# A sparse graph-attention block: hub stage, second-layer step order and norms rearranged

## The chip, the cores and the metric

The kernel runs on one core of a Trainium2 chip. Its time is the device time in microseconds of one launch, taken as the median over several runs. The core has a matrix engine (TensorE, PE in the profile; PEld is its weight load), VectorE (DVE), ScalarE (ACT), GpSimd (POOL) and SyncE (SP, which only issues transfers here). Each engine works through its own instructions in program order and waits on semaphores for the others. Transfers are issued from SP's, ACT's and POOL's queues.

## The reference

x is [8, 2048, 64]: 8 graphs over the same 2048 nodes with 64 features. adj is a 2048 x 2048 0/1 matrix that is very sparse, except that the first nodes (the hubs) have many neighbours. In essence:

```python
def gat(h, mask, b):                       # h: [..., N, D]
    scores = einsum('nd,md->nm', h, h)
    scores = where(mask, scores, -1e16)
    return einsum('nm,md->nd', softmax(scores), h) + b

mask = adj + eye(N) > 0
h   = einsum('bnc,hdc->bhnd', x, Wh)       # 4 heads of 64
z   = leaky_relu(concat_heads(gat(h, mask, bh)), 0.2)
h2  = einsum('bnk,dk->bnd', z, Wo)         # back to 64
z2  = leaky_relu(gat(h2, mask, bo), 0.2)
out = layernorm(x + (layernorm(z2) * gamma + beta))   # both without further weights
```

## The kernel before, in words

The kernel never forms the dense 2048 x 2048 attention. It splits the nodes into 56 hubs (HUB) and 1992 others, the others into 166 sets of 12 (SET, NS). For each set it finds the at most 128 nodes that are a neighbour of any of the 12, gathers just their rows, and computes a 128-wide attention with a mask. Hubs are done densely, in blocks of nodes. The 8 graphs are handled as 4 pairs (Q = 4), each pair side by side on the 128 partitions or columns.

All is emitted under `tc.manual_schedule()` (L1401): every engine runs its instructions in the order in which the Python code emits them, and only the waits are worked out. So the order of the lines is the order of the work. Four stages follow one another.

**Hub stage** (loop L958, 16 blocks i of 128 nodes). Before it, ACT's queue loads the x tiles 0 to 3 (`load_x`), SP's queue loads hub rows, weights and the first adjacency pieces; `hub_mask` and `hub_mask_sets` (L539, L556) build the hub masks maskh and maskt with PE transposes, `weights` turns the weight matrices, `hub_columns` makes the hubs' score columns yh. In each block `load_x(i + 4)` loads ahead, `more` loads adjacency pieces `raw` of 480 KB on SP and converts them on POOL to `a`, `save_x` writes the x tile to table1 on SP; then for two halves t, `hub_scores` (PE sh L590, DVE subtract e L594, ACT exp L597), the next block's transposes, `hub_values` of the half before (PE oh L608). `make_keys` (PE pk L721, DVE keys L708) packs adjacency columns into sort keys at fixed blocks; `pick` makes the list of selection jobs (DVE MAX8 and match-replace L737/739, index list, masks), of which `some(3)` runs three per half. When the list is empty the first gathers from table1 (POOL indirect transfers, L792) are issued.

**First layer** (loop L1017, steps i over 83 groups of two sets). A step computes scores of group i+1, values of group i, the output projection of i-1, second-layer maps of i-2 and rows of i-3, in one software pipeline. `keep_rows` (L892) adds the bias and stores the rows to table2 with two transfers on SP. `second_maps` and `second_rows` use corners of the step's PSUM tile `cat`.

**Passage and second layer** (loop L1351, steps u over NU = 42 groups of four sets). 24 gathers from table2 go out first (L1100), and tiles bd, es2, esh, ownb, linked are made and cleared on DVE (L1103 to L1117). `hub_block` (L1262) loads 120 rows of table2 for a hub block on SP. A step u emits, in this order:

- `scores2(u+2)` (PE s L1133, ACT exp into eT L1136); `values2(u)` (PE o L1165). Two steps share one o tile, and after the odd one `spread` puts that pair's norm jobs on the steps ahead.
- for a hub block, `hub_values2` (PE oh L1299); four gathers for u+6; `work_on(u, 0)`: the norm jobs of this step's first half; `roots(u)`: ACT Ln and Exp for the variances; `hub_lift2` (DVE L1285, ACT exp L1288) for the block whose scores were made the step before; `spread_own(u+3)`: ACT copies the sets' own columns into bd (L1124).
- `turn_scores(u+1)` (PE e L1144) and `keep_scores` (DVE es L1152); `turn2(u+4)`: two PSUM tiles with 8 transposes each (PE t L512), each copied by ACT to xTg (L1320); for a hub block `hub_scores2` (PE sh L1277); `work_on(u, 1)`.

Hub blocks fall on every second step from u = 2 (`hub_at`, L1346). The tiles of `turn2` and of `hub_scores2` share the tag "T", with two buffers in PSUM:

```python
tp = bank2(f"t2_{g}", "T", 2)             # turn2, two per step
sp = held["sh", b] = bank2(f"sh2_{b}", "T", 2)   # hub_scores2, read in hub_lift2
```

A norm (L1171) is: reciprocal and product with the softmax sums (`first`), leaky (`act`), sum, centre with a square on ACT, variance; scale, times gamma, plus the residual (`again`); and a second mean, centre, variance, scale and store. The jobs lie on eight successive steps, each list as (first half, second half):

```python
return [([], [first, act, mean(0)]), ([centre(0)], []), ([var(0)], []), ([], [again, mean(1)]), ([centre(1)], []),
        ([], []), ([var(1)], []), ([end], [])]
```

**End**: the loop runs seven steps past the last values so that the norms finish; eight stores per norm go out on SP (the last norm's partly on ACT). A flag tells whether a dense fallback must run; it doesn't here.

Of the kernel before, what the change touches and what calls it, by code (L numbers as in the profile page):

```python
# [359 lines left out]
def fast_kernel(ctx: ExitStack, tc: tile.TileContext, x, adj, Wh, bh, Wo, bo, gamma, beta, out, flag):  # L360
# [54 lines left out]
    wnat = early.tile([P, H, C], F32, name="wnat")  # L415
    whT = early.tile([P, H * D], F32, name="whT")
    gram = early.tile([P, H, P], F32, name="gram")
    wos = early.tile([D, H * D], F32, name="wos")
# [30 lines left out]
    def load_x(i):  # L449
        t = xrow[i] = rows_tile(f"x{i}")  # L450
        nc.vector.memset(t[:, :, 0:PW:PW - 1], 1.0)
        for p in range(2):
            nc.scalar.dma_start(out=t[:, :, 1 + p * D:1 + (p + 1) * D],
                                in_=x[p::2, i * P:(i + 1) * P, :].rearrange("q n c -> n q c"))
# [32 lines left out]
    number = early.tile([P, 2, HALFN], U16, name="number")  # L487
    nc.gpsimd.iota(number, [[1, 2], [2, SEG // 2], [SEG, HALFN // (SEG // 2)]], base=0, channel_multiplier=0)
    load_x(2)
    load_x(3)  # L490
# [18 lines left out]
    def turn(tp, rows):  # L509

        for q in range(Q):
            nc.tensor.transpose(tp[:, q * P:(q + 1) * P], rows[:, q, 1:1 + P], ident)  # L512
# [24 lines left out]
    HV = HW // 4  # L537

    def hub_mask():  # L539
# [3 lines left out]
        pm = two("pm")  # L543
# [3 lines left out]
        for k in range(2):  # L547
            nc.vector.tensor_scalar(
                maskh[:, k * 8:(k + 1) * 8, :].rearrange("p m (n h) -> p (m n) h", h=H),
                pm[:, k, :8 * HUB].unsqueeze(2).to_broadcast([P, 8 * HUB, H]), 0.0, 255.0, OP.is_equal, OP.mult)  # L550
# [5 lines left out]
    def hub_mask_sets():  # L556
        pm = two("pms")
        cols = early.tile([HUB, NS * SET], BF16, tag="a", name="hubs", bufs=5)
        nc.scalar.copy(cols.rearrange("n (s k) -> n s k", k=SET), hubm[:, HUB:].rearrange("n (k s) -> n s k", s=NS))
# [9 lines left out]
    yh = early.tile([P, 2, 2 * HUB * H], F32, name="yh")  # L569
# [29 lines left out]
    hubo = [two(f"oh{t}", "o") for t in range(2)]  # L599
# [63 lines left out]
    keys = [early.tile([P, HALFN], F32, name=f"keys{k}") for k in range(2)]  # L663
    cand = early.tile([P, SEG * KEEP], F32, name="cand")
    best = early.tile([P, P], F32, name="best")
# [226 lines left out]
    def keep_rows(g, pr):  # L892
# [3 lines left out]
        for j in range(2):  # L896
            nc.sync.dma_start(out=dst[2 * g + j], in_=r[j * 48:(j + 1) * 48])
# [41 lines left out]
    more(2)  # L939
    hub_mask()  # L940
    hub_mask_sets()
    weights()
    turn_x(0)
    hub_columns()
    picks = []

# [7 lines left out]

    for e in es:
        nc.vector.memset(e[:, 4 * HW:], 1.0)
    pend = None
    for i in range(NB):  # L958
        if i + 4 < NB:
            load_x(i + 4)  # L960
        more(2 if i < 7 else 1)
        save_x(i)
# [12 lines left out]
        for t in range(2):  # L975
# [6 lines left out]
            if t == 1 and i in (3, 6):  # L982
                make_keys(0, (i - 3) // 3, two)
                if i == 6:
                    picks = pick(0)
            if t == 1 and i in (9, 15):
                make_keys(1, (i - 9) // 6, two)
            some(3)
    hub_values(*pend)
    while picks:  # L990
        picks.pop(0)()
    LOOK = 5
    for g in range(LOOK - 2):
        for j in range(2):
            gather(table1, 2 * g + j, 1, rows_tile)
# [16 lines left out]

    picks = pick(1)
# [3 lines left out]
    for i in range(-4, NG + 3):  # L1017
# [6 lines left out]
        cat = one(f"cat{i}", "C")  # L1024
# [15 lines left out]
        if i + 6 < NG and i % 2 == 0 and i >= -2:  # L1040
            own_rows((i + 6) // 2)
        if 0 <= (i - 30) // 2 <= NV:
# [18 lines left out]
        if 0 <= i - 2 < NG:  # L1061
            second_maps(i - 2, cat[:, 0, 384:384 + GM])
        if 0 <= i - 3 < NG:
            second_rows(i - 3, cat[:GM, 1, 384:512])
        if 0 <= i + 4 < NG + NG % 2:
            columns(i + 4, cat)
        if 0 <= i - 2 < NG:
            keep_own(i - 2, cat[:, 0, 384:384 + GM])
        if 0 <= i - 3 < NG:
            keep_rows(i - 3, cat[:GM, 1, 384:512])  # L1070
# [13 lines left out]
    assert not picks and not pieces and not todo3 and done == NS  # L1084
# [13 lines left out]
    NU = (NS + 3) // 4  # L1098
    sets = [list(range(4 * u, min(4 * u + 4, NS))) for u in range(NU)]
# [3 lines left out]
    bd = [late.tile([P, 4, Q, 32], F32, name=f"bd{k}", bufs=1) for k in range(3)]  # L1103
    es2 = [late.tile([P, 2 * Q, 4, 32], F32, name=f"es2_{k}", bufs=1) for k in range(2)]
    esh = [late.tile([P, Q * 2 * HUB + 8], F32, name=f"esh{k}", bufs=1) for k in range(2)]
# [328 lines left out]
```

## Time and profile before

| | us |
|---|---|
| median of 9 runs | 880.39 (876.9 to 882.74) |
| the profiled execution | 878.06 |
| its span | 876.2 |
| mean granted PE clock | 0.957 |

| stage of the profiled execution | from | to |
|---|---|---|
| hub stage | 0 | 144.5 |
| first layer | 144.5 | 599.0 |
| passage to the second layer | 599.0 | 609.1 |
| second layer, up to the last values o | 609.1 | 843.83 |
| end | 843.83 | 876.2 |

The profile is of one execution. Each line of a group or of the timeline names the source line, the engine, the operation and the tiles (out<-in); a bracket at its end tells how long the engine was idle before it and what released it. In a row of stages stand the length, then the busy time of PE, PEld, DVE, ACT and POOL with the number of instructions, the granted PE clock, the share of DMA engines busy and GB/s.

### The profile page before, as it was taken

The page shows a single profiled execution, that of the slowest core. Times are in us where ns is not written, and L with a number is a line of the kernel's source. Part 1 is how long each engine was busy: PE and PEld are TensorE (multiplying, and loading weights), DVE is VectorE, ACT ScalarE, POOL GpSimd, SP SyncE. Part 2 cuts the span into 40 slices and gives each one's busy share as a digit, 9 for nine tenths or more (in the row PEclk, how much of TensorE's full clock was granted, in tenths as well). Part 3 has the DMA queues.
Part 4 walks back from the last instruction along what each step waited for, and adds up shares of the span by engine and source line. Part 5 has one row for each costly group of instructions (what it writes and reads, how often), then busy time and mean ns, then how long its engine had stood idle before and what let it go on. Part 6 is the DMA issues. An engine that isn't in the chain of part 4 may idle for free.

```text
span 876.2 us, 42066 instructions
## 1 busy us (share of the span) xinstructions
PE 748.6 (85%) x18437; PEld 657.4 (75%) x18437; DVE 610.1 (70%) x1369; ACT 514.1 (59%) x961; POOL 467.9 (53%) x612
## 2 busy tenths in 40 slices
PE   2895677889999999999999999993999999998730
PEld 2663456778778999988999999971889999988720
DVE  3346983568888778877655555553258999999994
ACT  2342333546556667666666667651677788887821
POOL 6643141448344546655666665503777777777300
PEclk9999999999999999999999999995999999999975
DMA  8787441356344445665566565513888888888611
GB/s 188 222 218 209 130 145 51 83 141 173 97 108 112 114 127 156 168 168 153 157 168 172 160 167 160 132 31 117 243 259 253 271 283 269 269 241 257 173 46 36
DMA packets 81794, 145.22 MB, mean 166 GB/s; under 512 B 30146, under 2 KB 46466, under 8 KB 81602
## 3 DMA queue, kind: packets, MB, share of 16 engines
q0 software_dynamic: 26720, 88.55, 36.6%
q1 hardware_dynamic: 37842, 49.65, 18.7%
q10 hardware_dynamic: 17040, 4.25, 2.6%
q8 instruction: 147, 2.41, 1.2%
q14 instruction: 45, 0.37, 0.1%
HBM read 123.91 MB, written 18.48 MB: 163 GB/s over the span
## 4 chain that ended last, share of the span: by engine, by line
PE 68%; DVE 13%; DMA 5%; ACT 5%; issue 5%; POOL 2%; SPq 1%; DVEq 0%; POOLq 0%; ACTq 0%
PE t L512 13%; PE s L821 10%; PE o L846 10%; PE cat L806 6%; PE s L1133 4%; PE o L863 4%; PE cat L531 4%; PE o L1165 3%; PE cat L880 3%; PE sh L1277 2%; PE e L1144 2%; PE cat L890 2%; ACT xTg L1320 2%; DMA g<-table,index 2%; DVE e L594 1%
## 5 line engine op out<-in xcount | busy, mean ns | idle before, releaser
L792 POOL DMA_INDIRECT g<-table,index x332 | 333.5, 1005 | 237.7 <-PE o L846 141.4
L512 PE MATMUL t<-ident,g 128*128 128x128 f32 x1328 | 182.7, 276 | 16.1 <-DMA gh<-table 10.4
L512 PEld LDWEIGHTS t<-ident,g 128*128 128x128 f32 x1328 | 155.5, 143 | 20.4 <-issue 13.6
L826 DVE TENSOR_TENSOR e<-s,mask 128x768 f32<-128x768 f32 x83 | 79.3, 956 | 86.3 <-PE s L821 82.8
L518 ACT ACTIVATE z<-cat,bhp 128x192 f32<-128x192 f32 x166 | 60.7, 417 | 84.7 <-PE cat L531 84.7
L846 PE MATMUL o<-g,e 128*64 128x65 f32 x2656 | 97.3, 227 | 0.0
L821 PEld LDWEIGHTS s<-y,xTg 64*64 64x64 f32 x5312 | 85.0, 135 | 13.8 <-issue 13.7
L821 PE MATMUL s<-y,xTg 64*64 64x48 f32 x5312 | 95.3, 221 | 0.0
L846 PEld LDWEIGHTS o<-g,e 128*64 128x64 f32 x2656 | 85.6, 139 | 9.9 <-issue 0.2
L1320 ACT COPY xTg<-t 128x1024 f32<-128x1024 f32 x83 | 80.2, 1016 | 17.6 <-PE t L512 17.1
L1030 ACT COPY xTg<-t 128x1024 f32<-128x1024 f32 x83 | 84.0, 1013 | 1.8 <-PE t L512 1.8
L833 ACT ACTIVATE e<-e,shifts 128x768 f32<-128x768 f32 x83 | 79.2, 954 | 2.1 <-DVE e L826 1.7
L812 ACT COPY y<-cat 128x384 f32<-128x384 f32 (+1 forms) x80 | 40.6, 507 | 63.5 <-PE o L863 40.9
L597 ACT ACTIVATE e<-e,shifts 128x896 f32<-128x896 f32 x32 | 33.4, 1042 | 75.3 <-DVE e L594 59.7
L680 POOL TENSOR_SCALAR a<-raw 120x1024 bf16<-120x1024 int32 (+1 forms) x34 | 38.0, 1122 | 62.6 <-DMA raw<-in_adj_dram 35.8
L806 PE MATMUL cat<-xo,gram 128*128 128x192 f32 (+1 forms) x320 | 65.0, 326 | 0.0
L853 DVE RECIPROCAL rall<-o 64x8 f32<-64x8 f32 x166 | 34.0, 205 | 40.9 <-PE o L846 39.6
L854 DVE TENSOR_TENSOR osb<-o,rall 128x512 f32<-128x512 f32 x83 | 57.4, 692 | 2.9
L806 PEld LDWEIGHTS cat<-xo,gram 128*128 128x128 f32 x320 | 53.2, 201 | 0.2
L1165 PE MATMUL o<-g,es 128*32 128x65 f32 x2656 | 48.1, 224 | 5.6 <-DVE y_s L1188 4.5
L594 DVE TENSOR_TENSOR e<-sh,maskh 128x896 f32<-128x896 f32 x32 | 34.8, 1087 | 25.8 <-PE sh L590 23.0
L1165 PEld LDWEIGHTS o<-g,es 128*32 128x32 f32 x2656 | 45.0, 112 | 6.7 <-issue 4.1
(177 smaller groups left out, 1375.2 us busy)
## 6 DMA issues: line engine op xcount, KB each, us to landing
raw<-in_adj_dram SPq DMA_DIRECT2D x32, 480.0 KB
table<-xb SPq DMA_DIRECT2D x22, 256.0 KB
xr_s<-table SPq DMA_DIRECT2D x21, 256.0 KB
g<-table,index POOLq DMA_INDIRECT x332
table<-x SPq DMA_DIRECT2D x16, 260.0 KB
x<-in_x_dram ACTq DMA_DIRECT2D x32, 128.0 KB
table<-rowt SPq DMA_DIRECT2D x166, 24.4 KB
xb<-in_x_dram SPq DMA_DIRECT2D x164, 24.0 KB
```

What stands on the lines that cost most here:

```text
L512: nc.tensor.transpose(tp[:, q * P:(q + 1) * P], rows[:, q, 1:1 + P], ident)
L518: nc.scalar.activation(z[:, hp], cat[:, :, hp * n:(hp + 1) * n], AF.Identity, bias=bhp[:, hp:hp + 1], scale=1.0)
L792: nc.gpsimd.indirect_dma_start(out=t.rearrange("n q c -> n (q c)"), out_offset=None, in_=table, in_offset=bass.IndirectOffsetOnAxis(ap=ind ...
L806: nc.tensor.matmul(cat[:, k, 2 * GM:2 * GM + n], gram[:, g % 2 * 2 + k, :], held["x", g // 2][:, :n], start=True, stop=True)
L821: nc.tensor.matmul(sp[half(r), p, (q * 2 + j) * M:(q * 2 + j + 1) * M], xt[half(p), j, q, half(r)], y[half(p), (j * Q + q) * M:(j * Q + q ...
L826: nc.vector.tensor_tensor(e[:, :16 * M].rearrange("p (a q n) -> p a q n", a=2, q=Q), sp[:, :, :8 * M].rearrange("p a (q n) -> p a q n", q= ...
L833: nc.scalar.activation(e[:, :16 * M], e[:, :16 * M], AF.Exp, bias=shifts[:, 0:1], scale=1.0)
L846: nc.tensor.matmul(op[half(p), j, o0:o0 + K1], e[:, c0:c0 + 64], rw[j][:, q, sums(p)], start=True, stop=True)
L854: nc.vector.tensor_tensor(osb, v[:, :, :, 1:K1], r.unsqueeze(3).to_broadcast([P, 4, 2, D]), OP.mult)
L1030: nc.scalar.copy(t, held.pop(("tp", i + 2)))
L1165: nc.tensor.matmul(op[t * 32:(t + 1) * 32, f, k * W2 + p:k * W2 + p + K1], e[:, 2 * q + p, k, :], rw[:, q, sums(p)], start=(a == 0 and k = ...
L1320: nc.scalar.copy(t, tp)
```

## The change

It has five parts.

1. Hub stage: several tiles live in six `share` tiles. `hub_mask_sets` moves from the start into block 1, and its column copy from ACT to DVE; the hub mask is made in two halves around `hub_columns`. x tiles 2 and 3 load on SP between adjacency pieces; the x tiles are saved later (`save_at`); pieces come in another rhythm. `make_keys(0, 1)` moves from block 6 to 8 and `make_keys(1, 0)` from 9 to 11; four selection jobs per half instead of three. The rest of the selection and the first gathers are emitted in block 14.
2. First layer: eleven jobs that clear and fill the second layer's tiles run at odd steps from 61 on (`ahead_of_second`), since those tiles now lie in `share` and in maskh. In the last steps ph and pr use their own PSUM tiles, and half of the last row stores are issued by ACT.
3. Second layer: the loop begins at u = -3 and transposes for u+3 instead of u+4. Gathers, the first half's norm jobs and `turn2` stand ahead of the hub part, `spread_own` and `turn_scores`; `roots` goes to the end of the step. The first hub loads wait for the transposes of the first gathers.
4. Norms: five steps instead of eight, with roots one and three steps after the start; a new norm's first jobs stand ahead of older norms' jobs of that half step.
5. The last norm's eight stores go over the queues of SP, ACT and POOL, and the loop ends two steps sooner.

```diff
@@ -415 +415,2 @@
-    wnat = early.tile([P, H, C], F32, name="wnat")
+    share = [const.tile([P, n], F32, name=f"share{k}") for k, n in enumerate([HALFN, HALFN, HALFN, 512, 512, 2 * 456])]
+    wnat = share[3][:, :H * C].rearrange("p (h c) -> p h c", h=H)
...
@@ -453 +454 @@
-            nc.scalar.dma_start(out=t[:, :, 1 + p * D:1 + (p + 1) * D],
+            (queue or nc.scalar).dma_start(out=t[:, :, 1 + p * D:1 + (p + 1) * D],
...
@@ -489,2 +489,0 @@
-    load_x(2)
-    load_x(3)
...
@@ -547,4 +549,5 @@
-        for k in range(2):
-            nc.vector.tensor_scalar(
-                maskh[:, k * 8:(k + 1) * 8, :].rearrange("p m (n h) -> p (m n) h", h=H),
-                pm[:, k, :8 * HUB].unsqueeze(2).to_broadcast([P, 8 * HUB, H]), 0.0, 255.0, OP.is_equal, OP.mult)
+    def hub_mask_half(k):
+        nc.vector.tensor_scalar(
+            maskh[:, k * 8:(k + 1) * 8, :].rearrange("p m (n h) -> p (m n) h", h=H),
+            maskp[0][:, k, :8 * HUB].unsqueeze(2).to_broadcast([P, 8 * HUB, H]), 0.0, 255.0, OP.is_equal, OP.mult)
@@ -559 +562 @@
-        nc.scalar.copy(cols.rearrange("n (s k) -> n s k", k=SET), hubm[:, HUB:].rearrange("n (k s) -> n s k", s=NS))
+        nc.vector.tensor_copy(cols.rearrange("n (s k) -> n s k", k=SET), hubm[:, HUB:].rearrange("n (k s) -> n s k", s=NS))
...
@@ -897 +900 @@
-            nc.sync.dma_start(out=dst[2 * g + j], in_=r[j * 48:(j + 1) * 48])
+            (nc.scalar if j and g >= NG - 2 else nc.sync).dma_start(out=dst[2 * g + j], in_=r[j * 48:(j + 1) * 48])
@@ -939 +942,4 @@
-    more(2)
+    more(1)
+    load_x(2, nc.sync)
+    more(1)
+    load_x(3, nc.sync)
@@ -941 +946,0 @@
-    hub_mask_sets()
@@ -942,0 +948 @@
+    hub_mask_half(0)
@@ -944,0 +951,2 @@
+    hub_mask_half(1)
+    hubo.extend(two(f"oh{t}", "o") for t in range(2))
@@ -945,0 +954 @@
+    save_at = {i: range(i - 5, i - 4) if i < 9 else range(2 * i - 14, 2 * i - 12) for i in range(5, 15)}
...
@@ -961,2 +971,3 @@
-        more(2 if i < 7 else 1)
-        save_x(i)
+        more(2 if i in (0, 2, 4) or 7 <= i < 13 else 1 if i < 7 else 0)
+        for k in save_at.get(i, ()):
+            save_x(k)
@@ -982,3 +993,3 @@
-            if t == 1 and i in (3, 6):
-                make_keys(0, (i - 3) // 3, two)
-                if i == 6:
+            if t == 1 and i in (3, 8):
+                make_keys(0, i // 8, two)
+                if i == 8:
@@ -986,3 +997,11 @@
-            if t == 1 and i in (9, 15):
-                make_keys(1, (i - 9) // 6, two)
-            some(3)
+            if t == 1 and i in (11, 15):
+                make_keys(1, i // 4 - 2, two)
+            if t == 1 and i == 1:
+                hub_mask_sets()
+            some(4)
+        if i == 14:
+            while picks:
+                picks.pop(0)()
+            for g in range(LOOK - 2):
+                for j in range(2):
+                    gather(table1, 2 * g + j, 1, rows_tile)
@@ -990,6 +1008,0 @@
-    while picks:
-        picks.pop(0)()
-    LOOK = 5
-    for g in range(LOOK - 2):
-        for j in range(2):
-            gather(table1, 2 * g + j, 1, rows_tile)
@@ -1012,0 +1026,31 @@
+    NU = (NS + 3) // 4
+    sets = [list(range(4 * u, min(4 * u + 4, NS))) for u in range(NU)]
+    bd = [t.rearrange("p (k q n) -> p k q n", k=4, q=Q) for t in (share[2][:, :512], share[2][:, 512:], share[4])]
+    es2 = [t.rearrange("p (b k n) -> p b k n", b=2 * Q, k=4) for t in share[:2]]
+    esh = [share[5][:, k * 456:(k + 1) * 456] for k in range(2)]
+    ownb = share[3][:, :Q * 2 * HUB].rearrange("c (q p n) -> c q p n", q=Q, p=2)
+    linked = maskh[:, 1:10, :].rearrange("p m n -> p (m n)")[:, :NS * SET].rearrange("p (s k) -> p s k", k=SET)
+    def spread_own(u):
+        w = len(sets[u])
+        for p in range(2):
+            src = own[half(p), :, sets[u][0] * SET:(sets[u][0] + w) * SET]
+            nc.scalar.copy(bd[u % 3][half(p), :w, :, 16 * p:16 * p + SET], src.rearrange("c q (k n) -> c k q n", k=w))
+    def clear_own():
+        nc.vector.memset(ownb, 0.0)
+        for p in range(2):
+            nc.vector.tensor_copy(ownb[half(p), :, p, :], ownh[half(p)].rearrange("c t (k n) -> c (t k) n", k=2))
+    def clear_ends():
+        for k in range(2):
+            nc.vector.memset(esh[k][:, Q * 2 * HUB:], 1.0)
+        nc.vector.memset(es2[0][:, :, :, 24:], 1.0)
+    def link():
+        nc.vector.tensor_scalar(linked, mask.rearrange("p s (k h) -> p s k h", h=H)[:, :, :, 0], 0.0, None, OP.is_equal)
+    ahead_of_second = ([clear_own] + [lambda t=t: nc.vector.memset(t, 0.0) for t in bd + es2] + [clear_ends, link] +
+                       [lambda u=u: spread_own(u) for u in range(3)])
@@ -1024 +1068,5 @@
-        cat = one(f"cat{i}", "C")
+        cat = one(f"cat{i}", "C") if i <= NG else None
+        if i < NG:
+            ph, pr = cat[:, 0, 384:384 + GM], cat[:GM, 1, 384:512]
+        else:
+            ph, pr = one(f"ph{i}", "S")[:, 0, :GM], one(f"pr{i}", "T")[:GM, 0, :P]
@@ -1041,0 +1090,2 @@
+        if i >= 60 and i % 2 and ahead_of_second:
+            ahead_of_second.pop(0)()
@@ -1062 +1112 @@
-            second_maps(i - 2, cat[:, 0, 384:384 + GM])
+            second_maps(i - 2, ph)
...
@@ -1103,22 +1150,0 @@
-    bd = [late.tile([P, 4, Q, 32], F32, name=f"bd{k}", bufs=1) for k in range(3)]
...
-    for p in range(2):
-        nc.vector.tensor_copy(ownb[half(p), :, p, :], ownh[half(p)].rearrange("c t (k n) -> c (t k) n", k=2))
-    for t in bd:
-        nc.vector.memset(t, 0.0)
-    for k in range(2):
-        nc.vector.memset(esh[k][:, Q * 2 * HUB:], 1.0)
-        nc.vector.memset(es2[k], 0.0)
-    nc.vector.memset(es2[0][:, :, :, 24:], 1.0)
...
@@ -1175 +1201 @@
-        at = [v + 2, v + 6]
+        at = [v + 1, v + 3]
@@ -1228,2 +1254 @@
-        return [([], [first, act, mean(0)]), ([centre(0)], []), ([var(0)], []), ([], [again, mean(1)]), ([centre(1)], []),
-                ([], []), ([var(1)], []), ([end], [])]
+        return [([first], [act]), ([mean(0), centre(0)], [var(0)]), ([again], [mean(1)]), ([centre(1)], [var(1)]), ([], [end])]
@@ -1248 +1273,2 @@
-                    (nc.scalar if v == NV - 1 and a else nc.sync).dma_start(out=dst, in_=y[p0:p0 + SET].rearrange("p (f w) c -> p f (w c)", f=2)[:, :, :w * D])
+                    queue = nc.sync if v < NV - 1 else (nc.sync, nc.scalar, nc.gpsimd)[(2 * t + a) % 3]
+                    queue.dma_start(out=dst, in_=y[p0:p0 + SET].rearrange("p (f w) c -> p f (w c)", f=2)[:, :, :w * D])
@@ -1262 +1288 @@
-    def hub_block(b):
+    def hub_block(b, behind=None):
@@ -1267 +1293,5 @@
-        nc.sync.dma_start(out=t.rearrange("n q c -> n (q c)")[:n], in_=src)
+        d = nc.sync.dma_start(out=t.rearrange("n q c -> n (q c)")[:n], in_=src)
+        if behind is not None:
+            tc.add_manual_dep(d.ins, behind.ins.name,
+                              mybir.DependencyInfo(mybir.DependencyClass.Sync, mybir.DependencyReason.DATA),
+                              reason="after the first gathers")
@@ -1308 +1338,2 @@
-                jobs.setdefault((u + k, t), []).extend(part[t])
+                now = jobs.setdefault((u + k, t), [])
+                now[:] = now + part[t] if k else part[t] + now
...
@@ -1346 +1377 @@
-    hub_at = {u: b for b, u in enumerate([-4, -3, -2, -1] + list(range(2, 2 * NHB, 2))[:NHB - 3])}
+    hub_at = {u: b for b, u in enumerate([-3, -2, -1] + list(range(2, 2 * NHB, 2))[:NHB - 2])}
@@ -1348,4 +1379 @@
-    for b in range(4):
-        hub_block(b)
-    spread_own(0)
-    for u in range(-4, NU + 7):
+    for u in range(-3, NU + 5):
@@ -1360,0 +1389,8 @@
+        for s in sets[u + 6] if 0 <= u < NU - 6 else []:
+            gather(table2, s, 2, rows2)
+        work_on(u, 0)
+        if u + 3 < NU:
+            turn2(u + 3)
+        if u in (-3, -2):
+            for k in range(2):
+                hub_block(2 * (u + 3) + k, held["at", 4 * (u + 3) + 2 * k + 1])
@@ -1367,5 +1403 @@
-                spread(u, norm_hub(u, oh2))
-        for s in sets[u + 6] if 0 <= u < NU - 6 else []:
-            gather(table2, s, 2, rows2)
-        work_on(u, 0)
-        roots(u)
+                spread(u + 2, norm_hub(u + 2, oh2))
@@ -1374 +1406 @@
-        if 0 <= u + 3 < NU and u > -3:
+        if 3 <= u + 3 < NU and u >= 0:
@@ -1383,2 +1414,0 @@
-        if u + 4 < NU:
-            turn2(u + 4)
@@ -1388 +1418,2 @@
-        if u == -3:
+        roots(u)
+        if u == -2:
```

## The prediction

> **What bounds the kernel now.** I read the page first (busy shares, chain that ended last), then busy time by stage, the order of work in a steady pair of second-layer steps, the waits there, and last the start, the passage between the layers and the end.
>
> ```profile
> span 876.2 us, 42066 instructions
> PE 748.6 (85%) x18437; PEld 657.4 (75%) x18437; DVE 610.1 (70%) x1369; ACT 514.1 (59%) x961; POOL 467.9 (53%) x612
> PE 68%; DVE 13%; DMA 5%; ACT 5%; issue 5%; POOL 2%; SPq 1%; DVEq 0%; POOLq 0%; ACTq 0%
> ```
>
> PE makes 68% of the chain, but not everywhere. By stage (PE, weight loads, DVE, ACT, POOL busy; clock):
>
> ```profile
> 0.00:144.50 144.50, 98.46 (x1734) 70.55 (x1734) 85.56 (x181) 46.41 (x52) 58.92 (x124) 0.98 0.64 172
> 144.50:599.00 454.50, 434.56 (x11455) 389.87 (x11455) 309.19 (x795) 286.35 (x588) 242.09 (x322) 0.99 0.50 134
> 599.00:609.10 10.10, 0.00 (x0) 0.03 (x1) 5.07 (x13) 0.70 (x2) 4.01 (x5) 0.50 0.41 121
> 708.00:718.50 10.50, 10.27 (x258) 9.50 (x257) 9.62 (x18) 8.61 (x15) 8.06 (x9) 1.00 0.90 277
> 843.80:876.20 32.40, 1.28 (x34) 0.94 (x34) 19.99 (x37) 4.78 (x13) 0.00 (x0) 0.50 0.18 40
> ```
>
> The row 708 to 718.5 is a steady pair of second-layer steps: PE 10.27 of 10.50, so nothing there can get much faster, and DVE, ACT and POOL are 77 to 92% full: a new order has no slack to hide in. The same pair in order of time:
>
> ```profile
> 697.48 1.93 ACT L1320 COPY xTg<-t 128x1024 f32<-128x1024 f32 x2 [0.25 <-PE t L512]
> 698.54 1.09 PE L1277 MATMUL sh<-ownb,own 128*120 128x112 f32 x8 [0.23 <-ACT xTg L1320]
> 699.57 1.08 PE L1133 MATMUL s<-xTg,bd 128*32 128x128 f32 x32
> 702.01 1.91 PE L512 MATMUL t<-ident,g 128*128 128x128 f32 x16
> 702.34 0.67 ACT L1288 ACTIVATE esh<-esh,shifts 120x448 f32<-120x448 f32 x1
> 702.91 0.69 ACT L1124 COPY bd<-own 64x192 f32<-64x192 f32 x2
> 703.63 1.93 ACT L1320 COPY xTg<-t 128x1024 f32<-128x1024 f32 x2
> 703.85 1.08 PE L1133 MATMUL s<-xTg,bd 128*32 128x128 f32 x32
> ```
>
> PE never waits but 0.23 at sh: the copies of transposed tiles serve a step later (lookahead 4), so s at 703.85 starts while ACT still copies. Spacings on PE: s 0.90, o 1.05, oh 0.62, e 0.49, two tiles of transposes 1.84, sh 1.03: 4.28 for the odd step, 5.93 for the even one. ACT spacings: copy 0.96, lift exp 0.57, bd 0.69.
>
> **The change, step by step.**
>
> *1 Hub stage, about 10.8 off.* These rows set the start:
>
> ```profile
> 13.01 3.58 ACT L559 COPY hubs<-hubm 56x1992 bf16<-56x1992 bf16 x1 [10.98 <-DMA x<-in_x_dram]
> 16.64 1.86 PE L562 MATMUL pms<-identb,hubs 56*120 56x56 bf16 x17 [8.86 <-ACT hubs L559]
> 30.65 1.09 DVE L594 TENSOR_TENSOR e<-sh,maskh 128x896 f32<-128x896 f32 x1 [1.04 <-PE sh L590]
> ```
>
> The set masks leave that chain: the weights' transposes, at 18.43 behind pms, move to about 9.9 (bounds: PE's pm ends 7.8; the x loads have landed 13.0), 8.5 earlier; first e at 22. In step 1 they come back as a DVE copy (1.2 to 3.58, nearest ACT's own 3.58 for it), PE 1.86, DVE 1.27: partly covered, I charge 2.5. Before, 14 subtracts and two key halves took 46.7 to 77.3 (PE 37.7 of it); with keys(0,1) two blocks later there are 18, so selection starts near 72.5. From there DVE is the bound, as in 77.3 to 126, where it was busy 45.1 of 48.7: 14 subtracts x 1.09, keys 2.4, some 29 of selection (45.1 less 13 subtracts and keys) are 47, with bubbles like those before 50 to 54: last subtract about 126.5 against 137.32. x2 and x3 now queue on SP between 480 KB pieces, saves come later, ACT's loads wait for DMA lanes they free: from a loss that leaves 3 of the gain to none, which gives 15.
>
> *2 Layer 1, about 2 lost.* Eleven jobs (clears 4.8 us, link 1.2, three spreads 0.69 each: 8.1 in all) go one per odd step into steps of 5.0 us, where PE is 434.56 of 454.50 busy and waits on ACT and DVE chains with about 0.3 spare. Bounds 0 and 8.1 - 11 x 0.3 = 4.8; taken 2, since DVE has a third free. What they leave, 603.42 to 609.87 on DVE, lay beside the first gathers and saves nothing by itself.
>
> *3 Passage, 2.5 off.* The four last row stores issue on SP in 2.83 us from 598.19; half go to ACT, 1.4 earlier, and two PE waits on rowt (0.71, 0.60) go with the separate banks, about 1.1:
>
> ```profile
> 598.19 2.83 SPq L897 DMA_DIRECT2D table<-rowt  x4
> 603.87 0.96 POOL L792 DMA_INDIRECT g<-table,index  x1 [5.57 <-DVE ownb L1107]
> ```
>
> So the first gather near 601.4; bounds 0 and 4. Less lookahead takes one filling step out: four gathers 1.25 apart, 5.0, plus hub loads that no longer stand ahead. Values of step 2, at 641.3 before, come near 633.4: 7.9 with the passage (bounds 5 and 9).
>
> *4 Second-layer steps, about 55 lost; this decides.* The transposes now come before the hub part and e, one step nearer their use; spread_own and hub_lift2 stand behind them, on ACT's queue too. There are two "T" buffers in PSUM. sh of an even step holds one until hub_lift2 in the next odd step, now behind the transposes: in the built program both transposed tiles of an odd step use the other, and the second waits for ACT's copy of the first (before, the lift went first and freed it). Odd step from s at 0: s to 0.90, o to 1.95, tile A; its copy starts 1.08 after it (3.03) and frees PE 1.06 later, 4.09; tile B, copy from 5.17 to 6.13; lift exp 0.58 (its DVE subtract, behind `first` and `again`, 0.44 + 0.73 + 3 x 0.73 from 2.1, ends at 6.0: just in time); spread 0.69, and PE 0.05 later. s of the next step needs that spread: 7.46 against 4.28. Even step: ACT squares wait for DVE's centre until 3.05, ending 3.56; two copies to 5.48, spread to 6.17; next s 6.23 against 5.93. Pair 13.69, taken 13.6; +3.1 over 10.51, 15 hub pairs: 46.5. What queues behind the late s is everything on PE; eT and es follow it. Without hub blocks (steps 32 to 38) both buffers are free, but DVE's about 10.1 plus the time until o is there stays in the loop: odd 6.1, even 7.0, 13.1; three pairs, +8.7. Bounds of the pair: 13.0, if squares and first cost nothing extra, and 14.0.
>
> What removes the 0.23 wait is worth 13 x 0.23 = 3.0 at most, and the pair above already contains it:
>
> ```profile
> PE sh L1277 <- ACT xTg L1320: 3.0, 13, 0.2
> ```
>
> The Trainium skill, page "Perfetto Trace Analysis", section "Matmuls", says that independent matmul groups should rotate through PSUM banks so that the evacuation of one overlaps the next. By it the shared buffer alone would cost the exposed round trip, 1.2 per pair, and the sum would be 24 rather than 55; the traced row (two tiles in 1.91 with ACT's copies beside) agrees with its premise, but the ACT queue behind the copy is mine.
>
> *5 End, 6.1 off.* Before, last o at 843.83 to the end: 32.4, of which DVE 19.99: four norms were in flight. After, five parts instead of eight leave two: the last one's own chain from o is 1.2 + DVE 9.0 + squares and roots 2.6 = 12.8; the other's rest 4.9 may lie beside it: 12.8 to 17.7, taken 17, plus 9.3 from the last y (866.9) to the end: 26.3. Stores on three queues: SP issued 28 of them in 19.5, beside the norms.
> The same skill, page "DMA: Bandwidth & Descriptors", section "Issuing engines are not separate DMA queues", says that this saves only issue time; by the row (four on ACT, 2.15) that is under 1.5, and the sum doesn't count it.
>
> Sum: -10.8 + 2 - 7.9 + 46.5 + 8.7 - 6.1 = +32.4. The profiled execution took 878.06 (span 876.2, 1.86 around it), 2.3 under the median 880.39; added to the median: 912.8, say 913. Parts' bounds (hub stage -4 to +8, layer 1 -2 to +2.8, pairs -11 to +7, passage and end +-3) give 895 to 930 for this case.
>
> **Rivals.**
> *Faster:* the odd step stays PE-bound because the copies and spread end in time. For it: ACT is only 8.61 of 10.5. Against: chain above is by queue order, not load. Pair 10.5: 880.4 - 22.8 = 857 (the sum without its two pair terms). It decides where the pair is under 10.5 + 22.8/20 = 11.65.
> *Even:* only the shared buffer costs, 1.2 for each of 20 pairs: 881; for it, the spread needs nothing of the copies but their queue; against, that queue is in order.
> *Hub stage gives nothing:* ACT's x loads stand behind lanes held by adj pieces, and its exps behind them (before: exps waited 7.9 on DMA saves): 924.
> *Selection or clears stall layer 1:* the full 4.8: 916, inside the range.
>
> **How the numbers follow.** Main case 0.70 (895 to 930), hub stage nothing 0.07, even 0.09, faster 0.14. To leave out no more than 2 in 10 the range runs from 874 to 934. About 0.3% (2.6 us) is what a measurement can tell from no change: the even case falls a third each way. Faster 0.17, same 0.03, slower 0.80.
>
> **What would show it.** Right: on PE, t waiting for ACT xTg once per odd step (about 1.2) and s waiting for ACT bd (2 or more) some 15 times; steady pair near 13.6 with PE under 80% busy; first e near 22; last o to end near 26. Wrong: a pair near 10.5 with no wait of s for bd (then faster), or a first e still near 30.

## The result, and the profile after

The changed kernel takes 935.14 us (median of 10 runs, 928.11 to 942.38), the kernel before 880.08 (31 runs): 1.0615 times as long, with a 95% interval of 1.0591 to 1.064. The forecast was slower, 913 within 874 to 934. The direction held; the time lies 1.1 us above the range. Ratios and intervals here and below leave out runs more than 1.5% above the fastest of their kernel, so they can differ a little from the quotient of the medians. The profiled execution took 936.02, its span is 933.7.

By stage, from the starts of the values o on PE, the first column product of the first layer and the first gather from table2 in the two profiled executions:

| stretch | before | after | difference | forecast |
|---|---|---|---|---|
| hub stage, to the first layer's first column product | 144.6 | 145.2 | +0.7 | -10.8 |
| first layer, from there to its last o | 444.3 | 452.1 | +7.8 | +2 |
| last o to the first gather of layer 2 | 15.1 | 12.1 | -3.0 | -2.5 |
| first gather to o of step 2 | 37.4 | 35.8 | -1.6 | -5.4 |
| o of step 2 to o of step 32 (hub blocks) | 159.4 | 202.5 | +43.2 | +46.5 |
| o of step 32 to the last o | 43.2 | 59.6 | +16.4 | +8.7 |
| last o to the end | 32.4 | 26.4 | -6.0 | -6.1 |
| sum | 876.2 | 933.7 | +57.5 | +32.4 |

First, the page of the kernel after: busy time by engine, and the chain that ended last.

```profile
span 933.7 us, 42051 instructions
PE 761.5 (82%) x18437; PEld 662.9 (71%) x18437; DVE 612.5 (66%) x1370; ACT 508.5 (54%) x958; POOL 466.6 (50%) x614
PE 53%; DVE 21%; DMA 8%; ACT 7%; issue 5%; POOL 3%; SPq 2%; DVEq 0%; POOLq 0%; ACTq 0%
```

The engines are busy for about as long as before (PE 761.5 against 748.6, the others within 6), but PE's share of the chain went from 68% to 53%, and DVE's from 13% to 21%: the queues of other engines now set more of the time.

Busy time by stretch of the kernel after (length; PE, PEld, DVE, ACT, POOL busy; clock; DMA share; GB/s): first layer, a pair of second-layer steps, the end.

```profile
145.20:605.70 460.50, 435.56 (x11455) 389.71 (x11455) 315.45 (x807) 288.31 (x594) 246.65 (x323) 0.99 0.49 133
711.30:724.90 13.60, 10.49 (x260) 9.40 (x260) 9.66 (x18) 8.51 (x15) 7.64 (x8) 1.00 0.77 213
907.30:933.70 26.40, 1.28 (x34) 0.94 (x34) 15.50 (x30) 3.78 (x10) 1.23 (x2) 0.50 0.16 37
```

The pair has nearly the same work as before (PE 10.49 against 10.27, DVE 9.66 against 9.62, ACT 8.51 against 8.61) in 13.6 us instead of 10.5. Here is its odd step in order of time, cut to the lines that carry it:

```profile
707.97 1.09 PE L511 MATMUL t<-ident,g 128*128 128x128 f32 x8 [1.10 <-ACT xTg L1351]
...
709.10 1.01 ACT L1351 COPY xTg<-t 128x1024 f32<-128x1024 f32 x1 [1.18 <-PE t L511]
709.35 0.62 DVE L1315 TENSOR_TENSOR share<-sh,maskt 120x448 f32<-120x448 f32 x1
709.89 0.55 DVE L1178 TENSOR_TENSOR share<-e,maskh 128x384 f32<-128x384 f32 x1
710.00 0.67 ACT L1318 ACTIVATE share<-share,shifts 120x448 f32<-120x448 f32 x1
710.58 0.70 ACT L1039 COPY share<-own 64x192 f32<-64x192 f32 x2
711.33 1.08 PE L1159 MATMUL s<-xTg,share 128*32 128x128 f32 x32 [1.83 <-ACT share L1039]
```

(DVE L1315 is the hub's subtract, DVE L1178 is es, ACT L1039 the spread; their tiles now lie in `share`.) PE waits 1.10 for the copy of the first transposed tile before it may write the second; that one's copy starts at 709.10, the hub's exp follows at 710.00, the spread at 710.58, and s can only start at 711.33, 1.83 idle. Before, both tiles ran in one stretch of 1.91. The loss lies in one half of the pair: from the o of an odd step to the next o it now takes 7.48 instead of 4.29, from the o of an even step 6.07 instead of 6.22. Over 660 to 830 us the waits of PE are:

```profile
PE s L1159 <- ACT share L1039: 20.9, 16, 1.8
PE t L511 <- ACT xTg L1351: 14.3, 13, 1.1
```

### The profile page after: what moved, and what is told of

It is laid out like the page before. It is cut to its first block, busy times and chain, and to the rows that moved or that the text cites. A ratio compares the mean times of both kernels' runs of the same rounds, so it can differ in the third digit from the quotient of the medians.

```text
span 933.7 us, 42051 instructions
## 1 busy us (share of the span) xinstructions
PE 761.5 (82%) x18437; PEld 662.9 (71%) x18437; DVE 612.5 (66%) x1370; ACT 508.5 (54%) x958; POOL 466.6 (50%) x614
## 4 chain that ended last, share of the span: by engine, by line
PE 53%; DVE 21%; DMA 8%; ACT 7%; issue 5%; POOL 3%; SPq 2%; DVEq 0%; POOLq 0%; ACTq 0%
PE t L511 9%; PE s L824 9%; PE o L849 9%; PE cat L809 5%; DMA raw<-in_adj_dram 5%; PE cat L531 4%; PE o L866 3%; ACT xTg L1351 3%; PE cat L883 3%; PE o L1191 3%; PE s L1159 3%; DVE y_s L1243 2%; DVE y_s L1228 2%; PE cat L893 2%; DVE st_s L1223 2%
## 5 line engine op out<-in xcount | busy, mean ns | idle before, releaser
L511 PE MATMUL t<-ident,g 128*128 128x128 f32 x1328 | 189.5, 279 | 30.0 <-ACT xTg L1351 16.5
L511 PEld LDWEIGHTS t<-ident,g 128*128 128x128 f32 x1328 | 153.1, 143 | 43.1 <-ACT xTg L1351 20.1
L849 PEld LDWEIGHTS o<-g,e 128*64 128x64 f32 x2656 | 84.3, 138 | 10.0 <-issue 0.3
L1159 PE MATMUL s<-xTg,share 128*32 128x128 f32 x1328 | 47.1, 284 | 47.8 <-ACT share L1039 41.0
L1159 PEld LDWEIGHTS s<-xTg,share 128*32 128x32 f32 x1328 | 35.2, 113 | 56.6 <-ACT share L1039 55.9
L1178 DVE TENSOR_TENSOR share<-e,maskh 128x384 f32<-128x384 f32 (+1 forms) x42 | 23.0, 547 | 48.4 <-PE e L1170 48.3
```

Source lines behind the costliest of these rows:

```text
L511: at = nc.tensor.transpose(tp[:, q * P:(q + 1) * P], rows[:, q, 1:1 + P], ident)
L849: nc.tensor.matmul(op[half(p), j, o0:o0 + K1], e[:, c0:c0 + 64], rw[j][:, q, sums(p)], start=True, stop=True)
L1159: nc.tensor.matmul(sp[q * 32:(q + 1) * 32, k, :], bd[u % 3][:, k, q, :], xt[:, s % 2, q, :], start=True, stop=True, tile_position=(0, q * 32))
```

## The experiments

Each kernel was measured beside the kernel before on the same chip, in five series. Three chips took 1040 to 1047 us for the kernel before instead of 880 ("chips at 1040" below, the others "chips at 880"). In one pair of the second layer, for instance, the granted PE clock there reads 0.83 with the changed loop and 0.90 with the old one, against 1.00 on a chip at 880, and PE idles in gaps that the profile puts down to issue; why was not found. So lengths are compared only among runs on chips at 1040, or only among runs on chips at 880. The pair is the mean from o of step 4 to o of step 30; each trace is of one execution.

**The changed kernel again.**

> The changed kernel itself, as the base of comparison on the chip of these experiments. If this chip is like those of the earlier experiments (kernel before near 1045, PE short of instructions in the second layer), the hub pair is near 20.3, the first layer starts near 154, and the ratio is 1.05 to 1.06; on a chip like that of the first measurement, pair 13.5 and 935.

Measured, on a chip that takes 879.42 for the kernel before: 932.55 us, ratio 1.0575 (1.0507 to 1.0644), pair 13.51 (in an execution of 942.49). The loss belongs to the kernel and not to the first chip.

**The second layer's loop as before**, in the changed kernel: the loop (order, lookahead, u from -4), the norm's eight parts and the last stores.

```diff
-    for u in range(-3, NU + 5):
+    for u in range(-4, NU + 7):
...
-        at = [v + 1, v + 3]
+        at = [v + 2, v + 6]
```

> The changed kernel, with the second layer's loop (order, lookahead 4, eight-part norms, end) as before; hub stage, first layer and early clearing as changed. If the step order is what costs (theory): first gather stays near 609.4, from there to the last o 240 as before (603.87 to 843.83) instead of 298, end 32.4 instead of 26.4; hub pair 10.5; time 884 +-4. Rival, that the shared tiles and their place cost and not the order: the pair stays at 13.5 and the time near 935 to 940.

On a chip at 1040: 1055.86 against 1047.05, ratio 1.0078 (1.0038 to 1.0117). The pair is 17.32 there; six runs that keep the changed loop are at 20.4 to 20.5 on such chips. So the loop with its norms, and not the tiles' new places, holds nearly all of the loss; what stays is under 1%, which this run doesn't divide further. It puts order, lookahead, norms and stores back together; the runs below part them.

**The hub part's subtract and exp ahead of the transposes.**

```diff
+        if u - 1 in hub_at:
+            hub_lift2(hub_at[u - 1])
         work_on(u, 0)
...
-        if u - 1 in hub_at:
-            hub_lift2(hub_at[u - 1])
```

> The changed kernel, with only the hub part's subtract and exp (hub_lift2) moved ahead of the first half's norm jobs and the transposes. Theory (two chains: the held buffer, then ACT's and DVE's queues): PE t no longer waits for ACT's copy, yet s still waits for the spread behind both copies and for es behind the norm jobs: hub pair 13.55 to about 12.2, 15 pairs, -20: 915. Rival A, the held buffer is all: pair 10.5, 890. Rival B, the buffer wait is hidden under ACT's queue: pair 13.5, 935.

On a chip at 1040: 1089.55 against 1047.05, ratio 1.0427 (1.0332 to 1.0522); pair 18.98 against 20.43 of a run on the same chip with the loop as changed: 1.45 less. In its trace t no longer waits for the copy. The edit also takes the hub's exp out of ACT's queue behind the copies, so the 1.45 is for the held buffer and the exp together; it is less than half of the 3.1 that the old loop gives back there.

**Subtract, exp and the spread copies ahead.** The same edit with `spread_own(u + 3)` moved along.

> The changed kernel, with the hub part's subtract and exp and the spread copies moved ahead of the first half's norm jobs and of the transposes, but es still behind those norm jobs. Theory (two further chains beside the buffer): es is late on DVE behind `first` and `again`, so the odd step gives back only part: against the changed kernel the pair falls by 1.0 to 1.5, as when the subtract alone was moved, and not by the 3.5 that came when es was freed too. Rival, the spread behind the copies is the whole rest: the pair falls by 3 or more.

On a chip at 880: 916.5 us, ratio 1.0405 (1.0341 to 1.0469). The pair is 12.68 against 13.52, with one idle stretch of 2.4 in step 4; from step 6 to 30 it is 12.52 against 13.53: 1.0 less. This run shows what is late next. Its waits of PE over 660 to 830 us, and the start of s in one odd step with the DVE work ahead of it:

```profile
PE s L1159 <- DVE share L1178: 24.2, 13, 1.9
PE sh L1307 <- ACT xTg L1351: 3.0, 13, 0.3
```

```profile
729.78 0.68 DVE L1243 TENSOR_TENSOR y_s<-y_s,var 128x512 f32<-128x512 f32 x1
730.07 0.60 PE L1170 MATMUL e<-ident,eT 128*128 128x128 f32 x4
730.50 0.69 DVE L1247 TENSOR_TENSOR y_s<-y_s,gam 128x512 f32<-128x512 f32 x1
731.23 0.69 DVE L1248 TENSOR_TENSOR y_s<-y_s,xr_s 128x512 f32<-128x512 f32 x1
731.84 0.55 DVE L1178 TENSOR_TENSOR share<-e,maskh 128x384 f32<-128x384 f32 x1
732.53 1.08 PE L1159 MATMUL s<-xTg,share 128*32 128x128 f32 x32 [1.86 <-DVE share L1178]
```

The waits of t and of s for ACT are gone. But the score transposes e start at 730.07, and es, which frees their PSUM tile for the next s (s and e share the tag "S2"), stands behind the three operations of a norm's `again` (scale, gamma, residual) and starts at 731.84; s waits 1.86, thirteen times alike.

**Subtract, exp, spread, and es ahead of the norm jobs.** As the last one, and `work_on(u, 0)` behind `keep_scores`. It ran three times, each time on a chip at 1040.

> The changed kernel, with the hub part's subtract and exp and the spread copies moved ahead of the transposes, and the first half's norm jobs moved behind the step's score transposes and es; lookahead stays 3. Theory (the odd step is late through the held buffer, the spread behind the copies on ACT, and es behind the norm jobs on DVE): all three go, s waits only for the second copy, odd step 7.5 to about 5.1, even 6.0: hub pair 11.1 instead of 13.55; 15 pairs, -37: 898. Rival, the lookahead of 3 is what costs, since copies then feed the very next s: pair 13 or more, 930.

> The changed kernel with lift, spread and es ahead of the first half's norm jobs, on a chip like that of the first measurement. Lift and spread alone gave a pair of 12.5 against 13.55. Theory: es behind the norm jobs is the rest; pair 11 to 11.3 (a second copy still ends behind PE's odd step), 15 pairs, -35: 900. Rival, es costs nothing: pair 12.5, 915.

> The changed kernel with lift, spread and es ahead of the first half's norm jobs. On a chip where the kernel before takes 880: theory pair 11 to 11.3, time near 900; rival (es costs nothing) pair 12.5, 915. Where it takes 1040: pair 16.9 as before, against 20.4 of the changed kernel.

Ratios 1.0086 (1.0049 to 1.0123), 1.0068 (1.0032 to 1.0104) and 1.0085 (1.0051 to 1.0119); pairs 16.96, 17.08 and 17.12, where the changed loop has 20.4 to 20.7 and the old loop 17.32. With three placements put right, and lookahead and norms still as changed, all of the pair's loss is gone there; s still waits for es (42.0 in 25 waits from 730 to 960 us in the first of the three). The time per pair on a chip at 880 stays unmeasured: 11 to 11.3 was forecast and no run shows it.

**Only the lookahead put back**, transposes for u+4 at the changed place, the loop from u = -4. It ran twice, on chips at 1040.

```diff
...
-        if u + 3 < NU:
-            turn2(u + 3)
+        if u + 4 < NU:
+            turn2(u + 4)
```

> The changed kernel, with only the lookahead put back: transposes for u+4 at the same place of the step, loop from -4. Theory (place in the step, not lookahead): the second tile still waits for the copy of the first and s still waits for the spread behind both copies: pair 13.3 to 13.6; one filling step more: 938. Rival, lookahead: s no longer waits, pair 10.5 to 11.7, 890 to 910.

> The changed kernel with only the lookahead of 4 put back. Theory (place in the step, not lookahead): pair 13.3 to 13.6, time 935 to 940. Rival: pair under 12.5, below 915.

Ratios 1.0571 (1.0502 to 1.064) and 1.0624 (1.0569 to 1.0679); pairs 20.70 and 20.61, no better than 20.4 to 20.5. On these chips less lookahead by itself costs nothing; the order within the step does.

**The clears behind the first layer** instead of in its steps. It ran twice, on chips at 1040.

```diff
-        if i >= 60 and i % 2 and ahead_of_second:
-            ahead_of_second.pop(0)()
...
+    while ahead_of_second:
+        ahead_of_second.pop(0)()
```

> The changed kernel, with the eleven clearing jobs taken out of the first layer's steps and run behind it. Theory (the jobs stall the first layer by 5): from the first layer's first column product to its last o 447 instead of 452; the clears then lie beside the landing of the last rows and the first gathers, so nothing is lost there: time 930. Rival, that the jobs are covered and the loss comes from elsewhere: 935; rival, that they delay the first s: 936 to 938.

> The changed kernel with the clears behind the first layer. Theory: from the first o to the last o of the first layer 435 to 436 instead of 440.5 (before 433.6), first gather 5 sooner, time 929. Rival, the clears cost nothing there: 440, 934.

1104.94 and 1097.72, ratios 1.0557 (1.0471 to 1.0644) and 1.0559 (1.0519 to 1.0599): too near those of the other runs with the changed loop (1.053 to 1.062) to tell by the median. In the traces the first layer from its first to its last o takes 459.6 and 456.0, against 461.9 to 466.7 and 460.2 to 462.7 in the three other runs of each series, which keep the clears in the steps: 2 to 7 less there. The trace of the changed kernel shows the mechanism; the first job goes in front of the step's own DVE work:

```profile
491.02 0.43 DVE L1042 MEMSET share<- 128x448 f32 x1
491.49 0.78 DVE L1044 COPY share<-ownh 64x224 f32<-64x224 f32 x2
492.30 1.61 DVE L523 SCALAR_TENSOR_TENSOR z<-z 128x384 f32<-128x384 f32 x1
...
494.36 0.50 ACT L815 COPY y<-cat 128x384 f32<-128x384 f32 x1 [3.12 <-DVE rowt L897]
494.75 0.54 ACT L873 COPY otb<-o 128x192 f32<-128x192 f32 x2
...
495.34 0.56 PE L531 MATMUL cat<-otb,whT 64*64 64x96 f32 x16 [1.99 <-ACT otb L873]
```

DVE hands the row on late, ACT's y and otb copies follow, and PE waits 1.99 in this step. Step by step against the kernel before, the values of layer 1 fall back by 3.5 until the jobs begin and by 8.5 when they are done: 5.0 of the 7.8 falls in the steps with the jobs. Chips at 880 bear this out: over steps 56 to 82 the run with subtract, exp and spread ahead loses 5.3 on the kernel before, and the last two versions below, with the clears behind the layer, lose nothing (0.6 gained and 0.0).

**x loads, saves and pieces in the rhythm of before.**

```diff
...
-        more(2 if i in (0, 2, 4) or 7 <= i < 13 else 1 if i < 7 else 0)
-        for k in save_at.get(i, ()):
-            save_x(k)
+        more(2 if i < 7 else 1)
+        if i < NB - 1:
+            save_x(i)
+        if i == NB - 2:
+            save_x(i + 1)
```

> The changed kernel, with x loads, x saves and adjacency pieces in the rhythm of before (x2 and x3 on ACT's queue at the start, x_i saved in block i, two pieces a block, then one); masks, keys and selection as changed. Theory (ACT's exps stood 21.1 us behind x loads that waited for a transfer lane): those waits fall below 10, first layer starts near 136 instead of 145.2, time 926. Rival, the later key blocks or the masks in block 1 hold the stage: start stays 143 to 147, time 935.

On a chip at 1040: 1107.22, ratio 1.0576 (1.0487 to 1.0665); the first layer starts at 153.8, and at 151.5 to 152.2 in the three others of that series. The theory fails in this form: the old rhythm has a stall of the same kind (ACT waits 6.4 for one save of x).

**x loads of the blocks on SP.** It ran three times, each time on a chip at 1040.

```diff
-            load_x(i + 4)
+            load_x(i + 4, nc.sync)
```

> The changed kernel, with the x loads of the hub stage's blocks issued on SP ahead of the block's adjacency pieces instead of on ACT. Theory (ACT's exps stand behind x loads that wait for a transfer lane; 21.1 us of ACT waits, of which some 8 reach PE): ACT no longer waits for x, selection starts near 73 instead of 81, first layer at 137 instead of 145, time 927. Rival, the volume of transfers or the pieces themselves pace the stage: first layer stays at 143 to 147, time 935.

> The changed kernel with the blocks' x loads on SP. Theory: selection starts near 77 instead of 82.9, first layer at 138 to 140 instead of 145.2 to 145.7, time 928. Rival, no gain where transfers are quick: 145, 934.

> The changed kernel with the blocks' x loads on SP. On a chip where the kernel before takes 880: first layer at 138 to 140 instead of 145.2, time 928; rival 145 and 934. Where it takes 1040: first layer at 147 to 150.5 as before, against 152 to 155.

Ratios 1.055 (1.0477 to 1.0623), 1.054 (1.0502 to 1.0578), 1.053 (1.0455 to 1.0605). The waits of ACT's exps for x are gone, and the first layer starts at 147.3, 150.5 and 148.8, where runs with the loads on ACT in the same series start at 154.8 to 155.0, 152.3 to 155.2 and 150.9: 2 to 8 sooner. Runs with the same hub stage differ by up to 3.4 within a series, so the size of the gain is rough. No run with this edit alone met a chip at 880. What the wait looks like in the changed kernel: ACT issues a load, and its exps stand behind it.

```profile
58.36 1.80 ACTq L454 DMA_DIRECT2D x<-in_x_dram  x2
60.21 1.04 ACT L600 ACTIVATE e<-e,shifts 128x896 f32<-128x896 f32 x1 [4.77 <-DMA x<-in_x_dram]
61.30 2.00 PE L611 MATMUL oh<-x,e 128*64 128x65 f32 x32 [3.57 <-ACT e L600]
65.14 1.09 DVE L597 TENSOR_TENSOR e<-sh,maskh 128x896 f32<-128x896 f32 x1 [6.16 <-PE sh L593]
```

**A version made of what held.** The changed kernel with the second layer as before, clears behind the first layer, x loads on SP:

> The changed kernel with the second layer's loop and norms as before, the clears behind the first layer, and the blocks' x loads on SP. If all three readings hold: first layer starts near 137 (before 144.5), takes 444 to its last o as before, the passage is 3 shorter than before, second layer 240 and end 32.4 as before: 865 to 870, ahead of the kernel before by 10 to 15. If x loads on SP give nothing: 875 to 878.

On a chip at 1040: 1038.04 against 1041.19, ratio 0.9953 (0.9919 to 0.9988); the first layer starts at 150.7, 4 sooner than in the two runs of that series with the loads on ACT. Then with the second half of the first keys in block 6 again:

```diff
...
-            if t == 1 and i in (3, 8):
+            if t == 1 and i in (3, 6):
```

> The combined version (second layer as before, clears behind the first layer, x on SP) with the second half of the first keys made in block 6 again instead of 8. Selection can then start two blocks (9) sooner, and DVE, which bounds the rest of the stage, idles less ahead of it: first layer starts 5 to 9 sooner than with block 8. If pieces aren't there by then (POOL waiting for them), nothing is gained. Time 0.985 to 0.99 of before.

On a chip at 880: 871.87 us, ratio 0.9916 (0.9881 to 0.9952). Its hub stage and its steady pair:

```profile
0.00:136.30 136.30, 99.46 (x1735) 72.00 (x1735) 89.34 (x182) 43.04 (x51) 60.51 (x123) 0.93 0.70 179
700.00:710.50 10.50, 10.27 (x272) 9.51 (x262) 9.63 (x18) 8.60 (x16) 8.05 (x9) 1.00 0.88 273
```

The pair is 10.56 with the tiles still in their new places, so on a chip at 880, too, the loss of the pairs belongs to the loop. The first layer takes 443.5 to its last o, as before (444.3). Selection starts at 64.9, where the changed kernel starts at 84.3, and the first layer at 136.3 instead of 145.2. Last, the mask sets' copy on POOL, their matmuls a block later:

> The same with the mask sets' column copy on POOL in block 1 and their matmuls and DVE part in block 2: the DVE copy of 2.9 and the wait for PE behind it leave the chain of block 1 (8.1 between subtracts there against 2.3 elsewhere): 3 to 5 sooner. If POOL's copy delays the pieces by as much, nothing.

870.02, ratio 0.9896 (0.9851 to 0.9941): its interval overlaps the last one's. Its first layer starts at 138.5, so the move gives nothing in the stage. Both versions are shorter than both kernels, than the kernel before by about 1%.

## Why the prediction was right or wrong

The sum is short by 25.1 us: 11.5 in the hub stage, 7.7 in the steps without hub blocks, 5.8 in the first layer and 3.8 in the fill, while the pairs cost 3.3 less than forecast and the passage gave 0.5 more.

**Second-layer steps with hub blocks (step 4): right in mechanism, within 8% in size.** The pair was put at 13.6 and is 13.52; its two halves were put at 7.46 and 6.23 and are 7.48 and 6.07. The waits named (t on the copy, s on the spread behind both copies) are the two lines shown above, 1.10 and 1.83. One thing was not priced: es. The prediction's "just in time" is for the hub's subtract behind `first` and `again`; es stands behind them, too. In the rows above es ends at 710.44, 0.84 before the spread, so it costs nothing there; with the buffer and the spread out of the way it sets the step by itself (12.52 instead of 10.50, s waiting 1.86). So taking one of the chains away gives only part of the loss back. The sum by the shared buffer alone was 1.2 per pair; PE's wait for it is 1.10 in the trace. The Trainium skill's advice on rotating PSUM banks (page "Perfetto Trace Analysis", section "Matmuls") agrees with that wait. The whole loss is 3.0 per pair, through the queues behind it.

**Steps without hub blocks: mis-sized, +16.4 instead of +8.7.** The three pairs from step 32 to 38, put at 13.1, take 14.6 (43.9 against 31.5 before): 3.8 of the missing 7.7. The steps from 38 to the last o, for which the sum has nothing, take 15.7 instead of 11.7: 4.0. The whole stretch before, and after:

```profile
800.66:843.83 43.17, 32.62 (x914) 29.04 (x906) 41.21 (x78) 29.40 (x57) 15.84 (x16) 0.94 0.55 153
```

```profile
847.69:907.30 59.61, 38.51 (x947) 34.66 (x938) 43.08 (x84) 30.70 (x59) 14.00 (x14) 0.88 0.39 105
```

DVE, which filled the stretch before (41.2 of 43.2), has hardly more to do after. PE waits 21.1 there for the spread and es, against 10.5 in all before, and it is busy 5.9 longer, at a granted clock of 0.88 against 0.94. The norm of the hubs, which the change puts on steps 34 to 38, can explain little of it: 8 of its 12 DVE operations (5.0 in all) lay in this stretch before, too, and the run with subtract, exp and spread ahead has the same norms and takes 53.2 there, at a clock of 0.97. What makes PE slower in this stretch was not tested.

**Hub stage (step 1): the step that failed, 11.5 of the 25 us that the sum is short.** The first subtract came as forecast, 20.9 for 22, and from the start of selection to the last subtract it took 53.7, for 54. What failed is between: "selection starts near 72.5". That allows 50.5 from the first subtract, for 18 subtracts, two key halves and the mask sets; it took 63.4, and selection starts at 84.3. The same stretch before (14 subtracts), and after (18):

```profile
30.65:77.31 46.66, 37.73 (x693) 26.02 (x693) 20.32 (x24) 17.69 (x21) 22.57 (x63) 0.96 0.77 213
```

```profile
20.88:84.31 63.43, 51.68 (x906) 37.52 (x906) 28.77 (x38) 22.77 (x27) 28.95 (x72) 0.87 0.75 194
```

The prediction doesn't write out how it comes to 50.5. PE's 37.7 for 14 subtracts makes 48.5 for 18, so the 50.5 is about PE's busy time, which is 51.7. The time in which PE idles, 8.9 before and 11.8 after, was put at nothing, without a reason. The 46.7 of the row scaled to 18 subtracts, plus the 2.5 for the masks, would have given 62.5. Most of the idle time is the rival that was given 0.07, ACT's exps behind x loads; PE waits for them

```profile
PE oh L611 <- ACT e L600: 7.2, 4, 3.6
```

in this stretch, and not at all in the first run with the loads on SP (on a chip at 1040), which needs 56.0 for it. The run with subtract, exp and spread ahead has the same hub stage, on a chip at 880: 61.4, with a wait of 4.9. On ACT's side the line is

```profile
ACT e L600 <- DMA x<-in_x_dram: 21.1, 5, 8.7
```

Of the 21.1, the 8.7 is ACT's idle time ahead of its first exp, which hurts nothing and is there with the loads on SP too; the stalls are 4.8 (shown above, at 60.21) and 5.8 (at 68.43). The mask sets cost 5.8 between two subtracts in block 1 (8.1 against 2.3 elsewhere) for the 2.5 charged. What the second keys in block 8 cost by themselves isn't shown: with block 6 and SP selection starts at 64.9, but from there to the last subtract it takes 64.2 instead of 53.7, and no run on a chip at 880 has SP with block 8.

**First layer (step 2): bound reached.** Taken 2, upper bound 4.8; the steps with the jobs lose 5.0, and nothing in the two versions without them. "DVE has a third free" did not count, because each job stands ahead of work that the same step waits for. Of the other 2.8, 0.9 is lost before the first o and the rest by step 42; what causes it was not tested.

**Passage and fill (step 3):** the passage gave 3.0 for 2.5; the fill 1.6 for 5.4. One filling step fewer did bring the first o nearer to the first gather, 23.5 instead of 27.6: 4.1. But the two steps from there to o of step 2 take 12.3 instead of 9.8: they are already steps of the new order, in which PE waits 1.8 for the spread and es and before waited for nothing, and the sum left this out.

**End (step 5):** 26.4, forecast 26.3: 17.5 from the last o to the last y, for 17, and 8.9 behind it, for 9.3. It may depend on the long pair, though: the three runs with five-step norms and the pair's loss gone need 28.2 to 29.1 (chips at 1040). The first of the two versions at 880 has the old norms and needs 32.1.

Of the rivals, the faster one fell, since the pair is 13.5, and the even one, since the shared buffer is not all. The other two came true, the hub stage that gives nothing and the full 4.8 in layer 1; each alone was within the range. The range itself was drawn narrower than its own parts: their bounds add to 893 to 934 around 912.8, and 895 to 930 was written for this case, without a reason.

## What to carry to other kernels

Where engines run in program order, price a reordering by each queue's order, not by busy shares: ACT was 63% busy in the late pair, and still PE waited for one of its last entries. When you scale a stretch from a row of the profile, scale its length and not the busy time of one engine, or say which waits go away: here that was 12 us of the hub stage. When a stall has several chains that end close together, taking one away shows the next; put all of them ahead before judging an idea (here, on chips at 1040, less lookahead costs nothing if the short steps that others wait for stand ahead of the long ones). Loads of x issued on ACT's queue made ACT's exps wait with them; issued on SP's queue, which has no computation, they did not.

## What the runs showed of the hardware that was not expected

Loads of x issued on ACT held that engine's exps for 4.8 and 5.8 us, although the data were wanted four blocks later; with the loads on SP no such wait shows. And chips differ: the same program took 880 on some and 1040 to 1047 on others. Most of it is in the second layer: from o of step 2 to the last o the first combined version takes 313.7 on a chip at 1040, and the one with the earlier keys, which has the same second layer, 203.4 on a chip at 880, 110 of the 173 by which their spans differ. Why was not found.
